# Where the slots of a scan kernel begin their convolutions, when a projection reuses a tile, and how much income a slot gets

## The chip, the cores and the metric

One core of a Trainium2 chip runs one program. The metric is the device time of one execution in microseconds. The kernel before takes 11173.16 us (median of three runs, 11170.04 to 11175.03).

## The reference

Eight images of 96 channels and 64 x 64 pixels pass two layers. The first normalizes, projects to 192 channels and a gate z, applies a depthwise 3 x 3 convolution and SiLU, and runs a selective scan in four directions: for each channel d and each of 16 states n, along the 4096 pixels,

```
dA = exp(delta * A)
h  = dA * h + (delta * u) * B
y  = sum over n of h * C
```

with `delta`, `B` and `C` projected from the convolved input. The four directions are summed, normalized, gated by silu(z) and projected back. A block of two 3 x 3 convolutions with a channel gate follows. The second layer is a linear attention over the 4096 tokens and a feed-forward net of 8-bit floats. What matters here: 8 x 4 x 192 x 16 recurrences of 4096 steps, and around them much smaller work whose results the scans need, or which needs the results of the scans.

## The kernel before, in words

**The scans.** Images go in four pairs (p = 0 to 3). A pair has four directions, four chunks of 1024 pixels and three tiles of 128 rows, so there are 192 jobs, and a job has 16 units of one 128 x 1024 tile each. Four units form a group, two a pair. For a unit VectorE multiplies `pu` by `bm` into `pb` and scans `da` and `pb` into `hc` (`scan`, line 1279); ScalarE makes `da` (`decay`, 1272); TensorE makes `pu`, once for a group of four units (`spread`, 1267, four rows in the trace); GpSimd multiplies `hc` by `cm`; and TensorE adds up the four units of the group before (`total`, 1315, the "sums": 32 rows on `yp`). The four products of a group read the same `pu`, so the next spread waits until the fourth product of the group is done, and the next group's first product waits for that spread. The loop is at line 1385. Every engine runs in the order in which the program is written (`InOrder`, 233, ties the instructions of TensorE, VectorE, ScalarE and GpSimd together); the DMAs all go through SyncE's queue.

**The slots.** All other work of the middle of the kernel is written as generators (lanes) that are given turns between the scans. `Slots.run` (304) is one turn, a slot. There is a slot before and a slot behind each pair of scans, so 4 slots in a group and 16 in a job; `slots.at` counts them. In a group the order is: spread and sums, then the first slot (`at % 4 == 0`), the second, the pair of scans with the decays of the pair after, the third slot, the fourth, the next pair of scans with the next decays, and then the next spread and sums. Since a slot has no length of its own, what a lane writes in the first slot stands on TensorE right behind the sums, and what it writes in the fourth stands right before the next spread.

**The income.** A lane that wants TensorE asks `take` (280) for one of two PSUM banks, `pg` in even slots and for long work, `yp` in odd ones, and says what it costs TensorE and ScalarE. Each slot adds RATE to two purses, up to CAP; `take` pays from them and gives nothing while a purse is empty. Long work (`long`, in slots) is only kept off the softplus slots 6 and 7 of a job (`due`).

**The lanes.** `before_scans` (986) prepares the pair to come: `norms` (1013), then `convs` (1090): for 512 pixels one projection `wz` of one matmul and two convolutions `wmain` and `wmix` of nine, three matmuls to a slot; each result is copied by ScalarE to a tile (`raw`, z first, to `u(0)`), SiLU follows in a third slot, four stores are queued one slot later, and `project` (1000) makes two more matmuls and copies their result to `u(0)` again, from which `xd` is stored; the next 512 pixels then copy their z to the same tile. `after_scans` (910) does the gate (553) and the `rest` (721) of the pair that is done: `norm2`, `squeeze` (677, a 3 x 3 convolution of 36 small matmuls in a piece, for which it holds one of two big tiles), a second convolution, the attention and the feed-forward net. `columns` (484) turns the sums of the vertical directions and holds both big tiles.

Ahead of the loop a first phase convolves what the first scans need; behind it a tail finishes the last pair.

Of the kernel before, what the change touches and what calls it, by code (L numbers as in the profile page):

```python
# [261 lines left out]
class Slots:  # L262
# [4 lines left out]

    RATE, CAP = (1.7, 1.7), (2.4, 2.4)  # L270

    def __init__(self, *banks):
        self.lanes, self.later, self.first, self.at, self.due = [], [], None, 0, {}
# [6 lines left out]
    def take(self, pe, act, long=0):  # L280
        while True:
            i = 1 if self.at % 2 and not long else 0

            due = self.at % 16 <= 6 < self.at % 16 + long
            if i not in self.held and not due and min(self.left) > 0:
                self.held.add(i)
                self.pay(pe, act)
                return self.banks[i]
            yield
# [32 lines left out]
def wait(n):  # L322
    for _ in range(n):
        yield


def phase_b(
# [8 lines left out]
    with ExitStack() as ctx:  # L336
# [87 lines left out]
        ]  # L424
        units = [(job, j, q) for job in range(len(jobs)) for j in range(4) for q in range(4)]
        carries, bcs, dus, dls, sts, das, hcs, prevs, yet = ({} for _ in range(9))
        turned, resting = set(), set()

        def where(job):
            p, k, ci, T = jobs[job]  # L430
# [53 lines left out]
        def columns(p):  # L484


            to = ys_d[0] if p else y_d
            yield from slots.take_big(0, 1)
            for T in (0, 2, 1):
                yc = []  # L490
                for i in range(2):
                    t = gp.tile([128, 2048], F32, name=f"big{i}")
                    nc.sync.dma_start(t, ys_d[1][p][T][:, 2048 * i : 2048 * i + 2048])
                    yc.append(t.rearrange("p (w h) -> p h w", h=H))

                def fetch(c):
                    t = gp.tile([128, 512], F32, name="turn", bufs=2)
                    at = slice(c * 512, c * 512 + 512)
                    nc.sync.dma_start(t, xi_d[0][p][T][:, at])
                    yr = None  # L500
                    if p == 0:
                        yr = unit(c % 2)[:, 0:512]
                        nc.sync.dma_start(yr, y_d[p][T][:, at])
                    return t, yr, at

                def store(t, at):
                    return lambda: nc.sync.dma_start(to[p][T][:, at], t)

                got = fetch(7)
                yield from wait(3)  # L510
                for c in range(7, -1, -1):
                    t, yr, at = got
                    if c:
                        got = fetch(c - 1)
                    se.mul(t, t, dsum[:, T : T + 1])
                    yield
                    for i in range(2):
                        v = t.rearrange("p (h w) -> p h w", w=W)[:, :, 32 * i : 32 * i + 32]
                        ge.tensor_add(v, v, yc[i][:, 8 * c : 8 * c + 8, :])
                    if yr is not None:  # L520
                        ge.tensor_add(t, t, yr)
                    slots.after(2, store(t, at))
                    yield from wait(2)
                yield
            slots.big.clear()
            yield from wait(2)
            turned.add(p)
# [149 lines left out]
        def squeeze(s, u, pieces):  # L677


            gpd = g_d[s].rearrange("c (h w) -> c h w", w=PH)  # L680
            yield from slots.take_big(s)
            for i in pieces:
                cin = gp.tile([128, 2048], F32, name=f"big{s}")[0:C, 0 : 18 * PH]
                nc.sync.dma_start(cin, u_d[s][:, 16 * i * PH : (16 * i + 18) * PH])
                cin = cin.rearrange("c (h w) -> c h w", w=PH)
                yield from wait(3)
                bank = yield from slots.take(1.2, 0.0, 4)
                for tap in range(9):
                    dy, dx = divmod(tap, 3)
                    for r in range(4):  # L690
                        pe.matmul(
                            bank[32 * r : 32 * r + 32, 0:256].rearrange("p (h w) -> p h w", w=W),
                            w1c[:, tap, :],
                            cin[:, 4 * r + dy : 4 * r + dy + 4, dx : dx + W],
                            start=(tap == 0),
                            stop=(tap == 8),
                        )
                    if dx == 2 and tap < 8:
                        yield
                        while tap == 5 and slots.at % 2:  # L700
                            yield
                        slots.pay(1.2, 0.0)
                g = u(2 + i % 2)[:, 0:256]
                slots.pay(0.0, 3.0)
                se.activation(g, bank[:, 0:256], AF.Gelu, bias=b1c)
                exps()
                slots.give(bank)
                for r in range(4):
                    r0 = 16 * i + 4 * r + 1
                    slots.after(  # L710
                        2,
                        put(
                            gpd[:, r0 : r0 + 4, 1 : W + 1],
                            g[32 * r : 32 * r + 32, :].rearrange("c (h w) -> c h w", w=W),
                        ),
                    )
                yield
            slots.big.remove(s)
            yield from wait(2)

        def rest(b, s):
# [184 lines left out]
                yield  # L906
            yield from wait(3)
            resting.remove(s)

        def after_scans(p):  # L910
            if p == 0:
                yield from columns(p)
            while resting:
                yield
            yield from gate(p, range(8))
            resting.update(range(2))
            for s in range(2):
                slots.lanes.append(rest(2 * p + s, s))

# [66 lines left out]
        def before_scans(p):  # L986
# [103 lines left out]
            def convs(b):  # L1090
# [20 lines left out]
                for j in js:  # L1111
                    if nxt is None:
                        while not there(j):
                            yield
                        nxt = fetch(j)
                        yield from wait(3)
                    x, nxt = nxt, None
                    raw = []
                    for i, w in enumerate((wz, wmain, wmix)):
                        bank = yield from slots.take(2.6 if i else 0.9, 0.0, 3 if i else 0)  # L1120
                        taps = 1 if i == 0 else 9
                        for t in range(taps):
                            dy, dx = divmod(t, 3) if i else (1, 1)
                            pe.matmul(
                                bank.rearrange("p (h w) -> p h w", w=W),
                                w[:, t, :],
                                x[:, dy : dy + 8, dx : dx + W],
                                start=(t == 0),
                                stop=(t == taps - 1),
                            )  # L1130
                            if t in (2, 5):
                                yield
                                slots.pay(2.6, 0.0)
                        raw.append(u(i)[:, 0:512])
                        slots.pay(0.0, 0.6)
                        se.copy(raw[i], bank)
                        slots.give(bank)
                        yield
                    if j < 7 and there(j + 1):
                        nxt = fetch(j + 1)  # L1140
                    z, main, mix = raw

                    while slots.at % 4 != 2 or slots.at % 16 == 6:
                        yield
                    slots.pay(0.0, 4.7)
                    se.activation(main, main, AF.Silu, bias=convb[:, 0:1])
                    se.activation(mix, mix, AF.Silu, bias=convb[:, 1:2])
                    se.activation(z, z, AF.Silu)
                    exps()
                    yield  # L1150
                    for dst, t in (
                        (xi_d[0][p][half], main),
                        (xi_d[0][p][2][rows, :], mix[0:64, :]),
                        (zs_d[p][half], z),
                        (zs_d[p][2][rows, :], mix[64:128, :]),
                    ):
                        slots.after(1, put(dst[:, ats[j]], t))
                    yield from project(0, b, main, mix, slice(0, 64), ats[j], u(0)[:, 0:512])
                    if not at_once:
                        rows_done.append(j)  # L1160
                    if j % 2:
                        slots.after(2, lambda j=j: rows_there(p, j // 2))
# [274 lines left out]
        p = NP - 1  # L1437
# [477 lines left out]
```

## Time and profile before

| | |
|---|---|
| time of the profiled execution | 11173.18 us |
| span, first to last instruction | 11171.2 us |
| first product of the scans begins | 227.1 us |
| last scan ends | 10830.8 us |
| VectorE busy | 10531.6 us (94%) |
| GpSimd busy | 9035.0 us (81%) |
| TensorE busy | 7943.3 us (71%) |
| ScalarE busy | 6601.8 us (59%) |
| 3072 products `pb` | 1213 ns each |
| 3072 scans `hc` | 2327 ns with a carry (2304), 2267 ns without (768) |

How to read it: nearly all instructions have the line of the recording helper (L245), so groups are told apart by their tiles, `out<-in`. A row "x32 | 1637.0, 411 | 27.5" is so many instructions, their busy time together, the mean of one in ns, and the engine's idle time just ahead of them, with the one that ended it. A fp32 matmul has two rows in the trace.

### The profile page before, as it was taken

To read this page: it belongs to the slowest core of one execution; us is meant where nothing else is said; L and a number is where in the kernel's file an instruction comes from. 1 tells how busy PE (TensorE), PEld (TensorE's weight loads), DVE (VectorE), ACT (ScalarE), POOL (GpSimd) and SP (SyncE) were. 2 spreads that over 40 slices of the span, in tenths; PEclk is the share of its full clock that TensorE was granted. 3 is DMA by queue.
4 is the path that set the end of the run, shared out by engine and by line. 5 is a ranking of instruction groups with operands and counts; after the bars stand their busy time and mean duration, and the time that the engine had idled before them with its cause. 6 is when DMAs were issued, how large, how long until landed. Compare 5 with 4: busy or idle time off the path is not lost.

```text
span 11171.2 us, 128095 instructions
## 1 busy us (share of the span) xinstructions
PE 7943.3 (71%) x39452; PEld 3134.6 (28%) x39452; DVE 10531.6 (94%) x6651; ACT 6601.8 (59%) x9179; POOL 9035.0 (81%) x6649
## 2 busy tenths in 40 slices
PE   7856777665578877667677877777667677665778
PEld 3312333222223332222222323222222233222223
DVE  4999999999999999999999999999999999999974
ACT  2545666444566666657666666666755655774554
POOL 2787878887898878998887887999889889997860
PEclk8877888877789888878788988888778787777889
DMA  3455545454555556665444565656545555554551
GB/s 115 147 177 172 161 149 159 157 190 131 165 189 172 157 159 204 202 196 187 151 147 159 166 159 162 224 183 205 165 139 170 150 173 177 183 168 129 177 157 37
DMA packets 900092, 1834.19 MB, mean 164 GB/s; under 512 B 247870, under 2 KB 421119, under 8 KB 892367
## 3 DMA queue, kind: packets, MB, share of 16 engines
q1 hardware_dynamic: 899406, 1826.01, 52.3%
q8 instruction: 313, 5.13, 0.2%
q14 instruction: 373, 3.05, 0.1%
HBM read 1405.13 MB, written 420.42 MB: 163 GB/s over the span
## 4 chain that ended last, share of the span: by engine, by line
PE 22%; issue 15%; DVE 10%; POOL 5%; ACT 4%; DMA 3%; SPq 0%; DVEq 0%; POOLq 0%; ACTq 0%
PE pu L245 8%; PE yp L245 8%; DVE hc L245 6%; PE pg L245 4%; DVE pb L245 4%; POOL hc L245 3%; ACT u L245 2%; PE t L245 2%; ACT da L245 1%; POOL u L245 1%; DMA bm<-xd 1%; DMA xd<-u 1%; POOL turn L245 0%; ACT w_dt.float L245 0%; ACT L245 0%
## 5 line engine op out<-in xcount | busy, mean ns | idle before, releaser
L245 POOL TENSOR_TENSOR hc<-hc,cm 128x1024 f32<-128x1024 f32 x3072 | 7233.6, 2360 | 623.3 <-DVE hc L245 403.1
L245 DVE TENSOR_TENSOR_SCAN hc<-da,carry,pb 128x1024 f32<-128x1024 f32 x2304 | 5269.1, 2327 | 77.0 <-ACT da L245 64.3
L245 PE MATMUL pu<-du,c_sel 128*128 128x512 f32 x3072 | 2415.6, 931 | 2237.1 <-DVE pb L245 2232.7
L245 DVE TENSOR_TENSOR pb<-pu,bm 128x1024 f32<-128x1024 f32 x3072 | 3590.8, 1213 | 185.9 <-PE pu L245 170.2
L245 ACT ACTIVATE da<-dl,c_alog 128x1024 f32<-128x1024 f32 x3072 | 3356.0, 1140 | 117.5 <-DVE hc L245 101.1
L245 ACT COPY y<-yp 128x256 f32<-128x256 f32 x768 | 284.7, 371 | 2622.2 <-PE yp L245 2493.3
L245 PEld LDWEIGHTS pu<-du,c_sel 128*128 128x128 f32 x3072 | 787.9, 279 | 3485.9 <-DVE pb L245 2715.8
L245 DVE TENSOR_TENSOR_SCAN hc<-da,pb 128x1024 f32<-128x1024 f32 x768 | 1709.9, 2267 | 27.9 <-ACT da L245 25.0
L245 PE MATMUL yp<-hc,c_add 128*32 128x256 f32 x24576 | 1637.0, 411 | 27.5 <-ACT u L245 9.7
L245 PEld LDWEIGHTS yp<-hc,c_add 128*32 128x32 f32 x24576 | 761.5, 119 | 1175.8 <-issue 595.9
L245 POOL COPY carry<-hc 128x1 f32<-128x1 f32 x2304 | 426.4, 185 | 785.1 <-DVE hc L245 743.3
L245 ACT ACT_TABLE_LOAD x566 | 726.2, 1283 | 26.6 <-DMA cb<-y 16.6
L245 POOL TENSOR_TENSOR u<-u,u 96x512 f32<-96x512 f32 (+1 forms) x426 | 538.3, 1270 | 98.5 <-ACT u L245 89.6
L245 ACT COPY u<-pg 128x512 f32<-128x512 f32 (+5 forms) x406 | 225.6, 556 | 633.2 <-PE pg L245 581.5
L245 POOL TENSOR_TENSOR du<-du,dls 128x1024 f32<-128x1024 f32 x192 | 453.6, 2362 | 131.6 <-ACT dls L245 128.9
L245 PE MATMUL pg<-ain,wmain 96*128 96x512 f32 x792 | 392.2, 646 | 44.3 <-ACT u L245 40.3
L245 ACT COPY u<-yp 96x512 f32<-96x512 f32 (+5 forms) x338 | 180.7, 535 | 399.3 <-PE yp L245 304.3
L245 PE MATMUL pg<-ain,wmix 96*128 96x512 f32 x792 | 376.1, 624 | 23.0 <-ACT u L245 20.2
L245 PE MATMUL yp<-prev,ident 128*128 128x256 f32 x768 | 316.3, 504 | 29.8 <-ACT dls L245 16.2
L245 PEld LDWEIGHTS yp<-prev,ident 128*128 128x128 f32 x768 | 211.7, 279 | 363.3 <-issue 258.6
L245 PE MATMUL yp<-st,dtw 12*128 12x512 f32 x384 | 234.3, 692 | 36.0 <-ACT u L245 24.4
L245 PE MATMUL pg<-st,dtw 12*128 12x512 f32 x384 | 222.6, 660 | 45.4 <-ACT u L245 25.8
(336 smaller groups left out, 7122.8 us busy)
## 6 DMA issues: line engine op xcount, KB each, us to landing
dl<-dl SPq DMA_DIRECT2D x768, 512.0 KB
bm<-xd SPq DMA_DIRECT2D x512, 512.0 KB
cm<-xd SPq DMA_DIRECT2D x512, 512.0 KB
du<-xi SPq DMA_DIRECT2D x192, 512.0 KB
dl<-dls SPq DMA_DIRECT2D x192, 512.0 KB
ya<-y SPq DMA_DIRECT2D x384, 128.0 KB
prev<-ya SPq DMA_DIRECT2D x384, 128.0 KB
xi<-u SPq DMA_DIRECT2D x152, 256.0 KB
```

Source lines behind the costliest of these rows:

```text
L245: op(*args, **kw)
```

## The change

Four edits.

1. In `take`, long work is given its bank only in the first slot of a group, behind the sums (work of two slots in the first or the second); it may begin with a purse as low as -2.
2. RATE goes from (1.7, 1.7) to (2.0, 1.8) a slot, and CAP from (2.4, 2.4) to (3.0, 2.4), for TensorE and ScalarE.
3. In `convs`, two slots pass between the four stores and `project`.
4. `columns` of a later pair lets the squeezes of the pair before go first, for at most 64 slots; `squeezed_at` records which images are through.

```diff
-    RATE, CAP = (1.7, 1.7), (2.4, 2.4)
+    RATE, CAP = (2.0, 1.8), (3.0, 2.4)
...
-            due = self.at % 16 <= 6 < self.at % 16 + long
-            if i not in self.held and not due and min(self.left) > 0:
+            due = long and (
+                self.at % 4 > (long == 2) or self.at % 16 <= 6 < self.at % 16 + long
+            )
+            if i not in self.held and not due and min(self.left) > (-2 if long else 0):
...
-        turned, resting = set(), set()
+        turned, resting, squeezed_at = set(), set(), set()
...
+            latest = slots.at + 64
+            while p and resting and squeezed_at < resting and slots.at < latest:
+                yield
             yield from slots.take_big(0, 1)
...
             slots.big.remove(s)
+            squeezed_at.add(s)
             yield from wait(2)
...
             resting.remove(s)
+            squeezed_at.discard(s)
...
             resting.update(range(2))
+            squeezed_at.clear()
...
                         slots.after(1, put(dst[:, ats[j]], t))
+                    yield from wait(2)
                     yield from project(0, b, main, mix, slice(0, 64), ats[j], u(0)[:, 0:512])
```

## The prediction

> **What bounds the kernel now.** The page and a table of stretches first.
>
> ```profile
> span 11171.2 us, 128095 instructions
> ...
> PE 7943.3 (71%) x39452; PEld 3134.6 (28%) x39452; DVE 10531.6 (94%) x6651; ACT 6601.8 (59%) x9179; POOL 9035.0 (81%) x6649
> ```
>
> ```profile
> core 0: us, PE busy (x) PEld busy (x) DVE busy (x) ACT busy (x) POOL busy (x), PEclk, DMA share, GB/s
> 2000.00:2920.00 920.00, 516.44 (x2770) 205.98 (x2768) 919.54 (x550) 418.38 (x475) 742.29 (x523) 0.77 0.49 159
> 3300.00:4000.00 700.00, 565.17 (x2538) 214.32 (x2536) 662.30 (x394) 446.99 (x667) 576.99 (x416) 0.88 0.52 162
> ```
>
> DVE sets the pace: in a stretch without convolutions it is never idle, in one with convolutions and a gate it loses 38 us of 700. Second, what DVE waits for:
>
> ```profile
> DVE pb L245 <- PE pu L245: 170.2, 76, 12.3
> DVE hc L245 <- ACT da L245: 89.2, 63, 7.9
> DVE pb L245 <- DMA bm<-xd: 14.9, 9, 3.4
> DVE hc L245 <- PE yp L245: 12.7, 6, 5.4
> ```
>
> About 290 us, of which 9.9 lie ahead of the first product; **281 us** are in the loop (227.1 to 10830.8). Only these can go, since the change alters no instruction of DVE, neither the phase ahead nor the tail, and both programs run the same 3,072 slots: no scan is held for a lane in either. Third, the timeline of PE, then of DVE, around one late spread:
>
> ```profile
> 3633.40 0.64 PE L245 MATMUL yp<-ident,u 128*96 128x128 f32 x4
> 3636.63 0.48 PE L245 MATMUL pg<-small,gmean 96*96 96x4 f32 x2 [2.58 <-ACT u L245]
> 3639.47 5.49 PE L245 MATMUL pg<-ain,wmix 96*128 96x512 f32 x6 [2.36 <-ACT small L245]
> 3644.75 2.47 PE L245 MATMUL pu<-du,c_sel 128*128 128x512 f32 x4
> ...
> 3647.25 2.36 DVE L245 TENSOR_TENSOR pb<-pu,bm 128x1024 f32<-128x1024 f32 x2 [4.04 <-PE pu L245]
> ```
>
> A short matmul waits for ACT, then three taps in the fourth slot run at half rate behind the gap (5.49 us for 6 rows), and the spread, which could have begun at 3638.8, comes 6 us late. Where taps follow the sums without a gap, 12 rows take as long, and nothing is late:
>
> ```profile
> 3211.19 2.52 PE L245 MATMUL yp<-hc,c_add 128*32 128x256 f32 x32
> 3213.64 2.84 PE L245 MATMUL pg<-ain,wmix 96*128 96x512 f32 x6
> 3216.32 1.02 PE L245 MATMUL yp<-u,mean 96*96 96x512 f32 x2
> 3217.18 5.31 PE L245 MATMUL pg<-ain,wmix 96*128 96x512 f32 x12
> 3222.33 1.88 PE L245 MATMUL pu<-du,c_sel 128*128 128x512 f32 x4
> ```
>
> Fourth, ACT: its waits, and one of them in the timeline, ahead of two decays.
>
> ```profile
> ACT u L245 <- DMA xd<-u: 71.4, 15, 12.7
> ACT u L245 <- DMA zs<-u: 55.0, 12, 10.5
> ...
> 6036.75 0.59 ACT L245 COPY u<-yp 128x512 f32<-128x512 f32 x1 [12.65 <-DMA xd<-u]
> 6037.23 2.19 ACT L245 ACTIVATE da<-dl,c_alog 128x1024 f32<-128x1024 f32 x2
> ```
>
> These are tile reuses: the projection's copy waits for z's store (zs), the next z's copy for the projection's store (xd).
>
> **The change part by part.** I cut the loop into 765 frames, one from spread to spread (13.5 us: a job of 53.9 us has four), put DVE's idle time down to the frame whose PE or ACT work ended it, and sorted frames by where convolutions and squeezes have their taps, from the order of the two built programs:
>
> - taps in the fourth slot: 97 frames, 137.0 us (28 with taps there alone hold 86.3, 3.1 each; 39 that begin in the second slot 31.7, 0.81 each). After: none.
> - taps, but none in the fourth: 86 frames, 18.2 us (33 in exactly the first three: 3.9; 31 in the first two: 14.3). After: 138 frames, all in exactly the first three.
> - no taps: 582 frames, 119.7 us. After: 627.
> - the first frame: 5.7.
>
> *Edit 1* empties the first class. The 138 frames of the second at 18.2/86 = 0.21 us make 29 (bounds 0.12 and 14.3/31 = 0.46 each: 17 and 63). What stands in such a frame: spread 1.9, sums 2.5, taps 18 x 0.43 = 7.7, so 12.1 of 13.5 us, and the spread may be some 2.6 us late unseen (two scans of 2.3 less 1.9). The short matmuls that fill the rest are alike: a mean of 0.7 us in these frames after, 0.5 in the 33 before.
>
> *Edit 2* lets denser frames form. Frames without taps carry 2.7 us of short matmuls before and after; those with 6 us or more are 48 of 582 and 52 of 627. I cost it at nothing beyond the frames' own rate; what hides it is PE's 29% idle time. If the cover is gone, a rival below has the price.
>
> *Edit 3* and the tile. Of the 119.7 us, 40.7 come within 17 us behind an ACT wait for zs or xd; the rest, 79.0/582 = 0.136, times 627 is **85**. The waits I count anew. The order has the projection's copy two slots behind SiLU 19 times before, never after; three slots behind 13 and 41 times. Behind the 13, DVE idled 6.6 us, 0.5 each, so 41 make **20** (bounds: none, and ACT's whole wait, 23.8/13 = 1.8 each, 75). But edits 2 and 3 bring the next z's copy close: one slot behind the projection's 10 times before, **24 after**; two slots 4 and 8. All 10 waited, 5.8 us on ACT in the mean, and DVE idled 57.9 us behind them, 5.8 each. What sets the length is the store: the one above was issued at 6027.88 and let ACT go at 6036.75, 8.9 us, behind six 512 KB loads issued in the 8.3 us before. Eight of the ten stood in the second or fourth slot, directly ahead of decays, two ahead of taps in the fourth slot. After, 23 of 24 stand in the first or third, a slot further from the decays and with no taps to delay. The nearest row is a copy in the third slot at 6601.57 (waited 7.46): its first decay ended at 6604.2; DVE, without the taps' 12.26 us, would have wanted it at 6600.1; 4.1 late, of which 2.8 came from a zs wait just before. I take 1.5 each, **36**, and 1 for the eight at two slots, **8** (bounds none and 5.8 and 2.2: 0 and 157). No page of the profile prices a short landing. The Trainium skill (DMA: Bandwidth & Descriptors, section "Latency and other measured facts") gives about 2 us as the fixed cost of a DMA; the row disagrees, with 8.9; by the page these 44 us would be none and the sum 11,032.
>
> *SiLU and GELU* sit in the third slot with two table loads, in 35 of the 138 frames. ACT then has up to 7.5 us in the third and fourth slots, decays included, and it did so in 17 frames with taps before at 0.2 us each, which the rate holds.
>
> *Edit 4* moves the turns of `columns` and their DMAs in SP's queue: in the second pair from jobs 74.9 to 79.8 to jobs 77.4 to 82.3, in the third from 121.2 to 126.1 to 125.4 to 130.3. They are due at jobs 84 and 132, so nothing waits for them; cost nothing, and with that cover gone a wait of up to a job, 54 us, would show on DVE.
>
> DMA loads are the same instructions in SP's order; their 15 us of waits are in the rates.
>
> **Sum**: 5.7 + 85 + 29 + 20 + 44 = 184 us of idle time for 281, a gain of 97. The profiled execution took 11173.18 us (span 11171.2), as the median, 11173.16: 11173 - 97 = **11,076**. All bounds low: 108, 11,000; all high: 386, 11,278.
>
> **Rivals.**
> *The tile becomes the bound (slower).* Place: z's copy one or two slots behind the projection, ScalarE's queue, decays behind it. Price: 5.8 and 2.2 us as measured before, 157, and 1.8 for each zs wait, 75; with 119.7 for the rest, 352: **11,244**. It decides from 2.2 us for each of the 73 copies. For it: all ten waited. Against: ACT has a slot more, and the half-rate taps are gone.
> *Full frames (no change).* If 138 frames idle like those with taps from the second to the fourth slot, 0.81, they cost 112 in place of 29: **11,159**. For it: 12.1 of 13.5 us is taken and purses may go to -2. Against: the 33 frames.
> *The waits are hidden (faster).* With zs and xd at nothing: 120 idle, **11,012**. For it: the slot positions. Against: 8.9 us landings.
> *It doesn't do what it says*: income that is not needed. The order shows the taps moved, but equal slots mean that income alone gains nothing; without a gain from places 11,173.
>
> **How the numbers follow.** A measurement tells about 0.2% (22 us) from no change. Forecast (11,030 to 11,130) 0.57, hidden waits 0.16, full frames 0.12, tile 0.12, nothing 0.03. Full frames lie on the edge (0.05 faster, 0.06 same, 0.01 slower). Faster 0.57 + 0.16 + 0.05 = 0.78, same 0.09, slower 0.13. The range takes in the hidden waits and full frames and stops inside the tile's case, leaving out its 0.12 and some of the low end: 11,000 to 11,200.
>
> **What would show it.** Right: `pb <- PE pu` falls from 170 to under 90 us; convolution groups of 18 rows take about 8 us behind the sums, few of them at half rate; DVE's rows keep 1213 and 2327 ns; zs waits keep under 2 us each and xd waits rise above 15 in number, while `hc <- ACT da` stays near 90. Wrong: `hc <- ACT da` above 150 (tile), or spreads late behind 18 rows in the first three slots (full frames), or waits of a kind not listed, POOL's above all.

## The result, and the profile after

The changed kernel takes **11082.07 us** (median of five runs, 11079.99 to 11085.53) against 11173.17 us (11170.04 to 11176.86) before, a ratio of 0.992 [0.991, 0.9931]: 91 us faster, where 97 were forecast. In the profile PE is TensorE, DVE is VectorE, ACT is ScalarE, POOL is GpSimd and SP is SyncE. First the page: the span, and the engines' busy time.

```profile
span 11079.4 us, 128083 instructions
...
PE 7885.3 (71%) x39452; PEld 3125.2 (28%) x39452; DVE 10527.5 (95%) x6651; ACT 6602.3 (60%) x9179; POOL 9028.5 (81%) x6649
```

DVE, ACT and POOL did the same work within 7 us, so the span of 91.8 us less is waiting that went. The first product begins at 227.2 us, the last scan ends at 10740.5: the loop is 90.3 us shorter, the tail 1.6. Of the 281 us in which VectorE was idle in the loop, **194.1** are left. The table of stretches, with the columns of before:

```profile
2000.00:2920.00 920.00, 538.38 (x2827) 214.46 (x2831) 918.29 (x548) 415.10 (x473) 738.85 (x522) 0.76 0.50 161
3300.00:4000.00 700.00, 578.02 (x2629) 221.70 (x2628) 689.89 (x412) 464.68 (x714) 597.48 (x433) 0.86 0.54 169
```

In the stretch with convolutions and a gate, DVE now loses 10 us of 700 instead of 38. What DVE waits for, in us, times and the longest:

```profile
DVE pb L245 <- PE pu L245: 97.9, 43, 9.9
DVE hc L245 <- ACT da L245: 55.8, 46, 5.1
DVE pb L245 <- DMA bm<-xd: 24.2, 20, 5.9
DVE hc L245 <- PE yp L245: 20.3, 6, 6.9
```

The wait for a spread fell by 72 us and that for a decay by 33; loads and sums took 17 back. TensorE's timeline between two spreads shows a frame with taps as the forecast wanted it:

```profile
3202.11 2.03 PE L245 MATMUL yp<-hc,c_add 128*32 128x256 f32 x32
3204.07 2.84 PE L245 MATMUL pg<-ain,wmix 96*128 96x512 f32 x6
3206.75 0.25 PE L245 MATMUL yp<-small,gmean 96*96 96x4 f32 x2
3206.86 5.40 PE L245 MATMUL pg<-ain,wmix 96*128 96x512 f32 x12
3212.10 2.08 PE L245 MATMUL yp<-u,c_centres 128*128 128x512 f32 x4
3214.11 1.98 PE L245 MATMUL pu<-du,c_sel 128*128 128x512 f32 x4
```

Eighteen rows of taps stand behind the sums without a gap, take 8.2 us, and the spread is at the array at 3214.1. TensorE's idle time ahead of a large group of taps, in the groups of before (rows, busy us and mean ns, idle us and releasers):

```profile
L245 PE MATMUL pg<-ain,wmain 96*128 96x512 f32 x792 | 392.2, 646 | 44.3 <-ACT u L245 40.3 <-ACT small L245 3.2 <-ACT s L245 0.6
```

and of after:

```profile
L245 PE MATMUL pg<-ain,wmain 96*128 96x512 f32 x792 | 354.3, 599 | 0.0
```

These taps never stand behind an idle array any more, and a row costs 599 ns where it cost 646. Neighbouring rows of taps that begin over 0.7 us apart, which I call half rate, were 115 of 1824 and are 3 of 1882. ScalarE's two waits for the tile:

```profile
ACT u L245 <- DMA xd<-u: 93.7, 26, 8.8
...
ACT u L245 <- DMA zs<-u: 20.5, 6, 6.4
```

The wait for z's store fell (55.0 in 12) and that for the projection's rose (71.4 in 15), as its step said.

**Where it was given back.** By jobs, DVE's idle time fell in the stretches in which convolutions run: jobs 48 to 84 from 109 to 50 us, jobs 104 to 131 from 99 to 31. It rose by more than 5 us in two: jobs 84 to 96 from 15.8 to 30.1 and jobs 131 to 144 from 0.3 to 30.4. There are no taps there. The chain is seen in one frame of after, with DVE, PE and POOL mixed in order of time:

```profile
7631.38 2.36 POOL L245 TENSOR_TENSOR hc<-hc,cm 128x1024 f32<-128x1024 f32 x1
...
7633.68 1.19 POOL L245 COPY u<-big 128x256 f32<-128x256 f32 x2
...
7640.26 1.15 POOL L245 COPY u<-big 128x256 f32<-128x256 f32 x2
7641.38 2.59 POOL L245 TENSOR_TENSOR u<-u,u 96x512 f32<-96x512 f32 x2
...
7644.02 2.02 PE L245 MATMUL yp<-u,c_centre 96*96 96x512 f32 x2 [12.70 <-POOL u L245]
...
7645.83 3.62 PE L245 MATMUL pu<-du,c_sel 128*128 128x512 f32 x4
...
7649.49 2.36 DVE L245 TENSOR_TENSOR pb<-pu,bm 128x1024 f32<-128x1024 f32 x2 [6.82 <-PE pu L245]
```

The attention stage of the `rest` needs two sums on GpSimd (`u<-u,u`) before a matmul. GpSimd, hardly idle here, works its queue in order: scan products of 2.36 us, and between them the copies `u<-big` with which `before_scans` turns the next pair's input (function `turn`, 48 copies for a pass over three tiles). The matmul waits 12.7 us, the spread behind it on TensorE is late, and DVE loses 6.82. GpSimd is busy for 215 us of the 220 from 7440 to 7660, and was for 215 before too. What differs is its work. Its groups in that window before:

```profile
L245 POOL COPY u<-big 128x256 f32<-128x256 f32 x48 | 28.6, 626 | 0.0
L245 POOL TENSOR_TENSOR u<-u,u 96x512 f32<-96x512 f32 x9 | 11.4, 1271 | 0.2
```

and after:

```profile
L245 POOL COPY u<-big 128x256 f32<-128x256 f32 x44 | 26.0, 620 | 0.0
L245 POOL TENSOR_TENSOR u<-u,u 96x512 f32<-96x512 f32 x20 | 25.3, 1267 | 0.8
```

The turn was there before, but not beside so much of a rest. What TensorE waits for on GpSimd's tiles `u` and `tn` in the whole span is, before:

```profile
PE yp L245 <- POOL u L245: 33.6, 13, 5.9
...
PE pg L245 <- POOL tn L245: 21.8, 7, 6.9
PE pg L245 <- POOL u L245: 18.7, 5, 5.9
...
PE yp L245 <- POOL tn L245: 3.3, 2, 2.6
```

and after:

```profile
PE yp L245 <- POOL u L245: 48.4, 10, 12.7
PE pg L245 <- POOL u L245: 36.8, 12, 9.6
PE pg L245 <- POOL tn L245: 30.0, 7, 8.4
...
PE yp L245 <- POOL tn L245: 19.0, 4, 7.4
```

These four rows are 134 us, for 77 before. In jobs 131 to 144 alone TensorE's waits for GpSimd rose from 3.1 to 54.3 us.

### The profile page after: what moved, and what is told of

Read it like the earlier page. It is cut to its first block, busy times and chain, and to the rows that moved or that the text cites. A ratio compares the mean times of both kernels' runs of the same rounds, so it can differ in the third digit from the quotient of the medians.

```text
span 11079.4 us, 128083 instructions
## 1 busy us (share of the span) xinstructions
PE 7885.3 (71%) x39452; PEld 3125.2 (28%) x39452; DVE 10527.5 (95%) x6651; ACT 6602.3 (60%) x9179; POOL 9028.5 (81%) x6649
## 4 chain that ended last, share of the span: by engine, by line
PE 32%; issue 28%; DVE 16%; POOL 12%; ACT 6%; DMA 5%; SPq 0%; DVEq 0%; POOLq 0%; ACTq 0%
PE pu L245 12%; PE yp L245 11%; DVE hc L245 10%; POOL hc L245 8%; PE pg L245 6%; DVE pb L245 5%; ACT u L245 2%; ACT da L245 2%; PE t L245 2%; DMA bm<-xd 2%; POOL u L245 1%; PE ps L188 1%; POOL turn L245 1%; POOL carry L245 1%; POOL du L245 1%
## 5 line engine op out<-in xcount | busy, mean ns | idle before, releaser
L245 DVE TENSOR_TENSOR_SCAN hc<-da,carry,pb 128x1024 f32<-128x1024 f32 x2304 | 5271.8, 2330 | 40.3 <-ACT da L245 33.9
L245 PE MATMUL pu<-du,c_sel 128*128 128x512 f32 x3072 | 2445.2, 941 | 2273.5 <-DVE pb L245 2269.0
L245 DVE TENSOR_TENSOR pb<-pu,bm 128x1024 f32<-128x1024 f32 x3072 | 3594.5, 1216 | 124.1 <-PE pu L245 97.9
L245 DVE TENSOR_TENSOR_SCAN hc<-da,pb 128x1024 f32<-128x1024 f32 x768 | 1711.0, 2270 | 39.7 <-ACT da L245 21.9
L245 ACT COPY u<-pg 128x512 f32<-128x512 f32 (+6 forms) x397 | 218.2, 550 | 715.5 <-PE pg L245 642.0
L245 ACT COPY u<-yp 96x512 f32<-96x512 f32 (+6 forms) x347 | 188.0, 542 | 463.4 <-PE yp L245 399.5
L245 PE MATMUL pg<-ain,wmain 96*128 96x512 f32 x792 | 354.3, 599 | 0.0
L245 PE MATMUL pg<-ain,wmix 96*128 96x512 f32 x792 | 353.0, 598 | 0.0
```

The lines of the kernel that those rows point to most:

```text
L245: op(*args, **kw)
```

## The experiments

Each is compared with runs of the kernel before on the same chip. The medians of these runs lie between 11165.05 and 11174.71, so a difference between two experiments that were run at different times is uncertain by up to 10 us. The first eight ask what the slot in which taps begin, the tile and the income are each worth.

**Without the place** (edit 1 undone; edits 2, 3 and 4 stay).

```diff
-            due = long and (
-                self.at % 4 > (long == 2) or self.at % 16 <= 6 < self.at % 16 + long
-            )
-            if i not in self.held and not due and min(self.left) > (-2 if long else 0):
+            due = self.at % 16 <= 6 < self.at % 16 + long
+            if i not in self.held and not due and min(self.left) > 0:
```

> The change without edit 1: long work may begin in any slot again; income, pause and order as after. By the order 100 of 765 frames have taps in the fourth slot (97 before, none after). Place theory: they idle as before, 1.4 us each, 141 us, and with 0.2 for the other frames the loop idles about 275 us: about 11,165 us, all of the gain gone, and DVE's pb <- PE pu at 150 or more. Tile theory (ScalarE's waits for the stores of a reused tile set the time): z's copy one slot behind the projection 13 times in place of 24 and the pause kept, so no worse than after, 11,060 to 11,082.

Measured: 11245.19 us, 1.0062 [1.0045, 1.0079], 163 us above the changed kernel and 70 above before. One hundred frames have taps in the fourth slot, with 203.6 us of idle time, in which one wait of 9.9 us is for a load; before it was 97 with 137.0. Half-rate rows are back at 117 of 1803. Without the place the rest of the change loses time: with more income, 19 frames have taps in all four slots (50.1 us, that load's wait among them), for 5 (10.9) before.

**Everything long in the fourth slot.**

```diff
-                self.at % 4 > (long == 2) or self.at % 16 <= 6 < self.at % 16 + long
+                self.at % 4 != 3 or self.at % 16 <= 6 < self.at % 16 + long
```

> After, but long work begins only in the fourth slot of a group, right before the spread, in place of the first. 138 frames then have taps in the fourth slot, 59 of them there alone. Place theory: 59 x 3.1 + 79 x 0.75 + 627 x 0.2 = about 365 us idle, 11,255 us, slower than before. Tile theory: only 9 copies of z one slot behind the projection, so faster than after, about 11,060.

Measured: 11386.3 us, 1.0188 [1.0173, 1.0203]. 138 frames with taps in the fourth slot idle 318.9 us, half-rate rows are 261 of 1751. Work, income, pause and edit 4 are the same, and only the slot in which long work may begin was changed: 304 us between first and fourth. That tile reuse sets the time falls. The size was under-estimated: 61 frames have taps in the first, second and fourth slot (18 rows that begin at the end of one group run on into the next) and cost 2.7 us each, a class of which before has fewer than five frames.

**Everything long in the second slot.**

```diff
-                self.at % 4 > (long == 2) or self.at % 16 <= 6 < self.at % 16 + long
+                self.at % 4 != 1 or self.at % 16 <= 6 < self.at % 16 + long
```

> After, but long work begins only in the second slot of a group: taps in the second, third and fourth in 110 frames, none in the fourth alone. Prediction's price of such frames: 110 x 0.81 = 90 us in place of after's 18 for its 138, and the rest as after: about 11,150. If what counts is only that taps run without a gap, at full rate, 11,080 to 11,100. If the fourth slot costs 1.4 or more wherever the taps begin, as in the kernel without edit 1 (2.0), 11,220 or more.

Measured: 11134.48 us, 0.9974 [0.9964, 0.9984]. 110 frames from the second to the fourth slot idle 120.8 us, 1.1 each, for 0.81 in the class of before; 43 half-rate rows of 1864. First, second and fourth slot stand in order: 11,082, 11,134, 11,386.

**Without the pause** (edit 3 undone in the changed kernel).

```diff
-                    yield from wait(2)
                     yield from project(0, b, main, mix, slice(0, 64), ats[j], u(0)[:, 0:512])
```

> After without edit 3: no two slots between the stores and the projection. By the order the projection's copy is two slots behind SiLU 32 times (none after), and the next z's copy one slot behind the projection 31 times (24 after). Tile theory: 32 zs waits at about 1 us of DVE each and 7 more xd waits at 1.5, 40 us: about 11,120 us. Place theory: the taps stand as after, so 11,075 to 11,090.

Measured: 11130.04 us, 0.9959 [0.9944, 0.9974], 48 above the changed kernel. On ScalarE the waits for z's store are 48.9 us in 15 (20.5 in 6 with the pause) and those for the projection's 146.5 in 37 (93.7 in 26); DVE's idle time within 17 us behind such waits is 71.8 us for 41.0. So the pause is worth 48 us on top of the placing, but not all of it through the tile. Of the 44 us more that the loop idles, 31 come behind these waits. Another 23 lie in jobs 84 to 96 and 131 to 144, where TensorE's waits for GpSimd are 122.8 us for 101.5. The other stretches idle 10 us less.

**The pause alone, on the kernel before.**

```diff
+                    yield from wait(2)
                     yield from project(0, b, main, mix, slice(0, 64), ats[j], u(0)[:, 0:512])
```

> Before, with edit 3 alone: two slots between the stores and the projection. 86 frames with taps in the fourth slot (97), the projection's copy two slots behind SiLU never (19), the next z's copy one slot behind it 15 times (10). Tile theory: 19 waits for zs gone, 20 to 30 us, 5 more waits for xd at up to 5.8 us, 29 us: 11,150 to 11,185. Place theory: 11 fewer frames at 1.4, 11,155. If the 49 us that the pause was worth on top of the change hold here as well, 11,125.

Measured: 11192.94 us, 1.0017 [1.0007, 1.0026], an interval that lies above 1: no gain, and if anything a loss of 19 us. z's waits fall from 55.0 to 36.8 us, the projection's rise from 71.4 to 113.2 in the same 15 times, and of DVE's idle time within 17 us behind such waits 97 us lie in frames with taps in the fourth slot, 49 before. By these rows the pause pays only where such frames are gone.

**The income alone, on the kernel before.**

```diff
-    RATE, CAP = (1.7, 1.7), (2.4, 2.4)
+    RATE, CAP = (2.0, 1.8), (3.0, 2.4)
```

> Before, with edit 2 alone: RATE (2.0, 1.8) and CAP (3.0, 2.4). 97 frames with taps in the fourth slot, as before. The prediction costs the income at nothing: 11,160 to 11,190. The kernel without edit 1 took 11,245, 70 us more than before at 100 such frames, though it had the pause; if that is the income, which lets short work crowd the frames whose fourth slot holds taps, this takes 11,230 to 11,290.

Measured: 11250.67 us, 1.0071 [1.0056, 1.0086]; the idle time rises to 353.3 us. As before, 97 frames have taps in the fourth slot, but they idle 193.2 us for 137.0 (one wait of 9.9 us for a load among them), and 24 of them have taps in all four slots for 5. TensorE's timeline of a frame with taps in the fourth slot alone:

```profile
3180.14 0.48 PE L245 MATMUL yp<-small,gmean 96*96 96x4 f32 x2 [5.39 <-ACT u L245]
3180.49 5.47 PE L245 MATMUL pg<-ain,wmain 96*128 96x512 f32 x6
3185.75 2.75 PE L245 MATMUL pu<-du,c_sel 128*128 128x512 f32 x4
```

A short matmul needs ScalarE's result of a few slots ago, the array stands for 5.39 us, the taps that follow run at half rate (5.47 us for 6 rows), and the spread is late. More income puts more short work and more taps into such frames: by the written order 3.8 other matmuls and 12.1 taps in the mean, for 2.8 and 11.1 before.

**More income in the changed kernel.**

```diff
-    RATE, CAP = (2.0, 1.8), (3.0, 2.4)
+    RATE, CAP = (2.4, 2.2), (3.0, 2.8)
```

> After, with RATE (2.4, 2.2) and CAP (3.0, 2.8): more income still. Taps stand in exactly the first three slots in 138 frames, none in the fourth, as after. Income alone cost the kernel before 76 us. If it costs because short work crowds the frames whose fourth slot holds taps, it costs nothing here; and since the attention stages now begin at jobs 79 and 125 in place of 82 and 129, ahead of turn (83.6 and 131.6), the collision theory has the stretches 84 to 96 and 131 to 144 idle some 15 us each less: 11,045 to 11,065. If income crowds all frames alike, 11,120 to 11,150.

Measured: 11122.15 us, 0.9958 [0.9941, 0.9975], 40 above the changed kernel. The 138 frames with taps idle 80.1 us for 18.5. Half-rate rows stay at 3, so it isn't the array's rate; `hc <- ACT da` is 106.5 us for 55.8. In order of time:

```profile
6461.30 5.42 PE L245 MATMUL pg<-ain,wmain 96*128 96x512 f32 x12
...
6466.55 2.08 PE L245 MATMUL yp<-u,c_centres 128*128 128x512 f32 x4
...
6468.67 0.69 ACT L245 ACTIVATE u<-yp,eps 128x512 f32<-128x512 f32 x1 [6.85 <-PE yp L245]
6469.39 0.63 ACT L245 ACTIVATE u<-u 128x512 f32<-128x512 f32 x1
6469.92 2.18 ACT L245 ACTIVATE da<-dl,c_alog 128x1024 f32<-128x1024 f32 x2
6471.15 4.58 DVE L245 TENSOR_TENSOR_SCAN hc<-da,carry,pb 128x1024 f32<-128x1024 f32 x2 [4.43 <-ACT da L245]
```

Short work written behind twelve rows of taps leaves the array only at 6468.6; ScalarE has waited 6.85 us for it, the decays stand behind it in ScalarE's queue, and the scan is 4.43 late. This is the rival of full frames, in another guise: it reaches DVE through ScalarE's queue and not through the spread. It isn't the whole of the loss. Of the 62 us more that the frames with taps idle, 21 come within 17 us behind ScalarE's waits for the tile, and those for z's store rose from 20.5 us in 6 to 50.0 in 11. Jobs 131 to 144, where the rests begin some four jobs earlier and the turn stands where it stood, idle 5.6 us for 30.4.

**More room between projection and next z** (pairs 1 to 3; copies one slot apart fall from 24 to 3).

```diff
                     yield from project(0, b, main, mix, slice(0, 64), ats[j], u(0)[:, 0:512])
+                    if p:
+                        yield from wait(1)
```

> After, with one more slot between the projection and the next z in the three later preparations: the next z's copy stands one slot behind the projection 3 times (24), two slots 25 times (8). Tile theory at the prices of after (24 waits for xd, 89 us on ScalarE, with some 30 us of DVE behind them): two thirds of it go, 11,060. Place theory: 11,080.

Measured: 11082.78 us, 0.992 [0.9905, 0.9934]: nothing. The wait for the projection's store falls by 23 us on ScalarE (70.4 in 21): of the 25 copies now two slots apart 19 still wait, 66.9 us. DVE's idle time behind the tile's waits falls from 41 to 33 us, and its waits for loads rise from 24 to 32. So one slot more takes away only a quarter of the wait, and that quarter brought nothing; what the rest of it costs isn't shown.

The last three ask whether GpSimd's turn beside the attention stage is what gave time back.

**The rest waits for GpSimd later** (two more slots between the rest's two sums and their matmul).

```diff
-                yield from wait(2)
+                yield from wait(4)
```

> After, with four slots in place of two between GpSimd's two sums into the residual tile and the normalization of it in the attention stage of rest. PE's waits for POOL rose from 82 to 146 us from before to after. If they are what was left of the gain (the larger spreads late in jobs 84 to 87 and 132 to 135 stand behind them), PE's waits for POOL u fall from 85 to under 40 us and the time to about 11,050 us. If they lie beside other waits, 11,075 to 11,085, with the same late spreads behind ACT.

Measured: 11093.01 us, 0.9925 [0.991, 0.994], not told apart from the changed kernel. TensorE's waits for `u` fell from 85 to 19 us, those for `tn` rose from 49 to 86. Together they are 105 us for 134, yet jobs 131 to 144 still idle 29.8: largely one wait took the place of another, which fits a queue on GpSimd that is as long as before.

**The last preparation's turn 64 slots (four jobs) later**, behind the attention stage.

```diff
+            if p == 3:
+                yield from wait(64)
             yield from slots.take_big(0, 1)
             for T in (0, 2, 1):
```

> After, with the transposing copies of the last pair's preparation (turn, GpSimd, jobs 131.3 to 134.8) begun 64 slots later, behind the attention stage of the two rests (jobs 129 to 136), with which they stand now. No other instruction moves by much. Collision theory (what the change gave back in jobs 131 to 144, 30 us of idle time for 0.3 before, comes from GpSimd, 215 of 220 us busy there, which TensorE waits for): that stretch falls under 8 us idle, PE's waits for POOL by some 35 us, 11,055 us. If the two rests alone are too much for ScalarE or TensorE, it stays near 30 us and 11,080.

Measured: 11060.89 us, 0.9901 [0.9886, 0.9916]. Jobs 131 to 144 idle 10.2 us for 30.4, and the loop 177.2 for 194.1; other stretches move by 5 us at most. TensorE's waits for GpSimd in these jobs fall from 54.3 to 22.4 us and DVE's for a spread from 27.7 to 9.8, and DVE waits there for no load in either run. The collision is confirmed there, at 20 us. The interval of this ratio and that of the changed kernel overlap, so it is the stretch that carries the reading.

**Apart**: the third preparation's turn 64 slots later too, the last columns as well, and a little more income.

```diff
-    RATE, CAP = (2.0, 1.8), (3.0, 2.4)
+    RATE, CAP = (2.1, 1.9), (3.0, 2.4)
...
+            if p == 3:
+                yield from wait(64)
             latest = slots.at + 64
...
+            if p > 1:
+                yield from wait(64)
             yield from slots.take_big(0, 1)
```

> After, with turn begun 64 slots later in the third and the last preparation (to jobs 87.6 to 91.1 and 135.3 to 138.8), the last columns 64 slots later (173.2 to 178.1), and RATE (2.1, 1.9), so that GpSimd's copies stand behind the attention stages (82 to 88, 129 to 135, 163 to 171). Collision theory: from the 30, 30 and 18 us of idle time after in jobs 84 to 96, 131 to 144 and 160 to 176 some 50 us go: 11,030. If turn begun later only moves the waits to the feed-forward stage that follows: 11,060 to 11,080.

Measured: **11023.51 us**, 0.9871 [0.9857, 0.9886], faster than both kernels. Idle time in the loop is 138.7 us; jobs 84 to 96 hold 20.5 (30.1 in the changed kernel), jobs 131 to 144 7.2 (30.4), jobs 160 to 176 4.0 (18.2). What DVE and then what TensorE waits for:

```profile
DVE pb L245 <- PE pu L245: 63.6, 45, 9.6
```

```profile
PE yp L245 <- POOL u L245: 25.9, 11, 5.5
PE pg L245 <- POOL u L245: 22.0, 6, 7.2
PE pg L245 <- POOL tn L245: 21.7, 6, 6.2
...
PE yp L245 <- POOL tn L245: 10.6, 4, 3.3
```

GpSimd's rows are down from 134 to 80 us and the spread's wait from 97.9 to 63.6. Four things were changed at once (two turns, the columns and the income); only the last turn was tried by itself.

## Why the prediction was right, point by point

The mechanism of edit 1 held, and the time came within 6 us. How close it came is partly luck: one term of the sum was 53 us too low and the two before it together 42 too high. The sum's terms, set beside the same sorting of the trace of after:

| term, us of DVE's idle time | forecast | after |
|---|---|---|
| frames with taps in the fourth slot | 0 | 0 (none is left) |
| 138 frames with taps in the first three | 29 | 10.4 |
| behind waits for zs and xd, all frames | 64 | 41.0 |
| the rest of the frames without taps, loads included | 85 | 137.6 |
| first frame | 5.7 | 5.1 |
| sum | 184 | 194.1 |

- **Edit 1 was right and is the change.** Undone, with the other three in place, it costs 163 us; turned round to the fourth slot, 304. The rate of 0.21 us for a frame with taps in the first three slots was even too high: 18.5 us in 138 frames with the tile's part, 0.13 each. The rival of full frames (112) didn't come at this income.
- **The price of a fourth-slot frame isn't fixed.** It was 137.0/97 = 1.4 us before, about 2 with edits 2, 3 and 4, and 2.3 with all taps there. The forecast never needed it after the change, but the expectations for the fourth slot went by the prices of before and came out low.
- **Edit 2 at nothing was wrong as a step and harmless in the sum.** I named TensorE's 29% of idle time as the cover. By itself the income costs 76.5 us (11250.67 less 11174.16); TensorE's idle time isn't where the work goes. The cover is edit 1, which keeps taps from the end of the frame, and it is thin: at (2.4, 2.2) 40 us come back, most of it through ScalarE.
- **Edit 3 was right in kind and priced too high.** z's copy stands one slot behind the projection's 24 times, as counted; 19 of the 24 waited, 69.2 us on ScalarE, so 2.9 a copy where the ten of before had 5.8. Of the projection's 41 copies, which wait for z's store, 6 waited, 20.5 us on ScalarE, no more than the 20 forecast for DVE, though 3.4 for each that waits, not under 2. DVE idled 41 us behind all of them, for 64. The tile as the bound (11,244) falls; without the pause a part of it appears, and one slot more room brings nothing.
- **The mis-sized term is the frames without taps.** Their 0.136 us was taken over from before as if they were alike: 85 forecast, 137.6 measured, 53 more. Jobs 84 to 96 and 131 to 144 hold 44 us more than before, and there TensorE waits for GpSimd. I asked of each moved step what it waits for, and not beside which work the steps that nobody edited would come to stand: the turn and the rest both follow from when their lanes get slots. The prediction named waits for POOL as what would make it wrong; they came, on TensorE, and the smaller other terms (19 and 23 us) hid them in the sum, which ended 10 us above the forecast. Moving the last turn away took 20 us back in its stretch.
- **Signs that didn't hold:** `pb <- PE pu` is 97.9 and not under 90, for that reason; `hc <- ACT da` is 55.8 and not near 90, a gain that I had not counted. VectorE's rows kept their durations (1216, 2330 and 2270 ns).
- **Edit 4 isn't priced.** With the old income or without edit 4, the written order doesn't bring the vertical sums or the rests through before the direction or the gate that needs them, so edit 1 alone and the change without edit 4 weren't tried. What brought the rest beside the turn is edit 1 on top of the others: in the run without it, which keeps the other three, jobs 84 to 96 and 131 to 144 idle 0.0 and 0.6 us, and TensorE waits there for GpSimd not at all.

The Trainium skill (DMA: Bandwidth & Descriptors, section "Latency and other measured facts") gives about 2 us as the fixed cost of a DMA. By it the 44 us for the projection's store would have been none. The trace after still has 26 waits of up to 8.8 us for such a store, so the rows of before were the better guide.

## What to carry to other kernels

Where an engine runs in program order, ask of long work not how much of it fits, but what stands right behind it: placed behind work that the bound engine seldom waits for (the sums, 6 waits in all) it cost 0.1 us a frame here, placed before the instruction that the bound engine needs it cost 1.4 to 2.3. Price a moved placement for the steps that nobody edited as well: list, stretch by stretch, which of them now meet on an in-order engine that is nearly full. And an idle share of an engine is no cover for more work until the idle time is shown to lie where the work goes.

## What the runs showed of the hardware

Six rows of taps took 5.49 us behind gaps of 2.58 and 2.36 us that a short matmul of 0.48 us parted, and 2.84 us behind the sums: a gap ahead of long work is paid twice. With taps behind the sums alone, half-rate rows went from 115 to 3, while TensorE's busy share (71% in both) and its mean granted clock (0.820 before, 0.817 after) hardly changed.

The Trainium skill (TensorE: Matmul & The Clock Gate, section "What's actually happening") says that the array falls to half rate after an idle window of about 3.4 us. The gap of 5.39 us in the run with the income alone fits; the pair of 2.58 and 2.36 us is shorter each, and longer only together.
